# Four graph layers on one core: projections by one level of Strassen's algorithm over pairs of graphs, with every engine's order written by hand

## The chip, the core and the metric

The kernel runs on one core of a Trainium2 chip. The core has TensorE (PE in the profile; its weight loads are the row PEld), VectorE (DVE), ScalarE (ACT), GpSimd (POOL) and SyncE (SP), and 16 DMA engines. Each engine takes its own instructions in the order in which they stand in its queue, and semaphores order the engines against each other. The metric is device time in microseconds of one execution of the whole program. All data and all arithmetic are float32.

## The reference

There are 128 graphs of 128 nodes with 512 features. `x` is [128, 128, 512], `adj` is [128, 128, 128]. Four layers follow each other, each of them a residual with a layer normalisation, `LN(v) = (v - mean) / sqrt(var + 1e-5)` over the features:

```
An = D^-1/2 (adj + I) D^-1/2     with D the row sums of adj + I      (layers 0 and 3)
layer 0:  x = LN(x + relu(An x W0 + b0))
layer 1:  q, k = split(x Wqk^T)          v = x Wv^T
          w = softmax over nodes of sum_m (q k^T / 8 * adj)[n, m]
          x = LN(x + w * v)
layer 2:  agg = (adj x) / max(rowsum(adj), 1e-6)
          x = LN(x + relu([x, agg] W2^T))
layer 3:  x = LN(x + An (x W3 + b3))
```

W0, Wv and W3 are 512x512, W2^T is 1024x512, Wqk^T is 512x128. Per graph the projections are five products of [128, 512] by [512, 512]: one each in layers 0, 1 and 3 and two in layer 2.

## The kernel before, in words

Nodes lie on the 128 partitions. Four graphs make a group (G = 4), so there are 32 groups. The main loop runs `t` from 0 to 32; I call one turn of it a pass. In pass `t` group `t` goes through layers 0 and 1, and group `u = t - 1` through layers 2 and 3, so that two groups are in flight and one can fill the other's waits. `prep` for group `t + 1` sits in the middle of layer 3 of group `u`.

A layer is made of pieces. `aggregate` (L131) multiplies adjacency and features into a transposed result in a PSUM tile of pool `ps_t` (two buffers), four 128x128 products at a time, and ACT copies it to SBUF (L138). `transpose_x` (L141) does the same with the features alone (copy on L145). `project` (L147) takes four such chunks as the stationary operand and runs the weights past them, 512 columns at a time (L151), into one PSUM bank of `ps_big` (four buffers). DVE reads the bank, adds bias or applies the relu and adds the residual into a new tile of features (L184 and L185 for layer 0, L248 for layer 1, L265 for layer 2, L278 and L279 for layer 3). `stats` (L159) then takes the batch-norm statistics of that graph on DVE, and when the four graphs of the group are done `normalise` (L164) computes the reciprocal root for all four at once: a small DVE operation (L167), one power on POOL over 128x4 elements (L169), and four DVE operations in place (L171). A float32 product is two instructions on PE, a transpose is one.

The order of the instructions on each engine comes from the Tile framework, which starts from the order in the Python code and lets an instruction pass others on its engine (in the built program the row sums of `prep` for groups 1 and 2, for instance, stand on DVE ahead of layer 0 of group 0). ACT has only copies, the two scalings of q and k and the exponentials to do. POOL does the 160 small powers and issues the weight loads (L66, L71); SP issues the loads of `adj` and `x` (L55, L57) and the stores (L283).

Of the kernel before, what the change touches and what calls it, by code (L numbers as in the profile page):

```python
# [13 lines left out]
P = 128          # nodes of a graph, on the partitions  # L14
G = 4            # graphs handled together
F = 512          # features
C = F // P       # feature chunks of 128
ATT = 64
LN_EPS = 1e-5
DEG_EPS = 1e-6  # L20


@with_exitstack
def kernel(
# [4 lines left out]
    w0: bass.AP,      # [F, F]   in, out  # L29
    b0: bass.AP,      # [F]  # L30
    wqkT: bass.AP,    # [F, 2 * ATT]
    wvT: bass.AP,     # [F, F]   in, out
    w2T: bass.AP,     # [2 * F, F] in, out
    w3: bass.AP,      # [F, F]   in, out
    b3: bass.AP,      # [F]
# [7 lines left out]
    xp = ctx.enter_context(tc.tile_pool(name="xp", bufs=2))  # L43
    ap = ctx.enter_context(tc.tile_pool(name="ap", bufs=2))
    tp = ctx.enter_context(tc.tile_pool(name="tp", bufs=4))
    sp = ctx.enter_context(tc.tile_pool(name="sp", bufs=4))
    ps_big = ctx.enter_context(tc.tile_pool(name="ps_big", bufs=4, space=bass.MemoryType.PSUM))
    ps_t = ctx.enter_context(tc.tile_pool(name="ps_t", bufs=2, space=bass.MemoryType.PSUM))
    ps_s = ctx.enter_context(tc.tile_pool(name="ps_s", bufs=2, space=bass.MemoryType.PSUM))

    st = {}          # (name, group) -> tile

    def load(t):
        a = ap.tile([P, G, P], FP, tag="adj", name=f"adj_{t}", bufs=3)
        nc.sync.dma_start(a, adj[t * G:(t + 1) * G].rearrange("g n m -> n g m"))  # L55
        xi = xp.tile([P, G, F], FP, tag="x0", name=f"x0_{t}")
        nc.sync.dma_start(xi, x[t * G:(t + 1) * G].rearrange("g n f -> n g f"))  # L57
        st["adj", t], st["x0", t] = a, xi

# [1 line left out]
    load(0)  # L61

    def weight(src, name):
        n, m = src.shape
        w = const.tile([P, n // P, m], FP, tag=name, name=name)
        nc.gpsimd.dma_start(w, src.rearrange("(c p) m -> p c m", p=P))  # L66
        return w

# [11 lines left out]
    w0_sb = weight(w0, "w0_sb")  # L80
    b0_sb = broadcast_row(b0, "b0_sb")
    wqk_sb = weight(wqkT, "wqk_sb")
    wv_sb = weight(wvT, "wv_sb")
    w2_sb = weight(w2T, "w2_sb")
    w3_sb = weight(w3, "w3_sb")
# [6 lines left out]
    def prep(t):  # L92
# [3 lines left out]
        rdeg = sp.tile([P, G], FP, tag="rdeg", name=f"rdeg_{t}")  # L96
        nc.vector.tensor_scalar(rdeg, deg, DEG_EPS, None, ALU.max)
        nc.vector.reciprocal(rdeg, rdeg)
        ar = ap.tile([P, G, P], FP, tag="ar", name=f"ar_{t}")
        nc.vector.tensor_tensor(ar, a, per_graph(rdeg), ALU.mult)  # L100

# [4 lines left out]
        an = ap.tile([P, G, P], FP, tag="an", name=f"an_{t}")  # L106
        nc.vector.tensor_tensor(an, a, ident[:, None, :].to_broadcast([P, G, P]), ALU.add)
        nc.vector.tensor_tensor(an, an, per_graph(d), ALU.mult)

        p_r = ps_t.tile([P, G, P], FP, tag="pt", name=f"p_ar_{t}")  # L110
        for g in range(G):
            nc.tensor.transpose(p_r[:, g, :], ar[:, g, :], ident)  # L112
        arT = ap.tile([P, G, P], FP, tag="arT", name=f"arT_{t}", bufs=3)
        nc.scalar.copy(arT, p_r)
# [4 lines left out]
        nc.vector.tensor_tensor(anT, p_n, per_graph(d), ALU.mult)  # L119
        st["arT", t], st["anT", t] = arT, anT  # L120

    # row sums of An, which carry the bias of layer 3
    def row_sums(t):
        p = ps_s.tile([P, P], FP, tag="psm", name=f"p_rs_{t}")
        for g in range(G):
            nc.tensor.matmul(p[:, g:g + 1], st["anT", t][:, g, :], ones, start=True, stop=True)  # L126
        rs = sp.tile([P, G], FP, tag="rs", name=f"rs_{t}")
        nc.vector.tensor_copy(rs, p[:, :G])
        st["rs", t] = rs

# [1 line left out]
    def aggregate(name, t, g, xin, aT):  # L132
        """(A x)^T in chunks of 128 features, [f, node]."""
        p = ps_t.tile([P, C, P], FP, tag="pt", name=f"p_{name}_{t}_{g}")
        for c in range(C):
            nc.tensor.matmul(p[:, c, :], xin[:, g, c * P:(c + 1) * P], aT[:, g, :], start=True, stop=True)  # L136
        s = tp.tile([P, C, P], FP, tag="aggT", name=f"{name}_{t}_{g}", bufs=6)
        nc.scalar.copy(s, p)  # L138
        st[name, t, g] = s

    def transpose_x(name, t, g, xin, dst):  # L141
# [3 lines left out]
        nc.scalar.copy(dst, p)  # L145

    def project(name, t, g, parts):  # L147
        """sum over (lhsT chunks, weight chunks) -> PSUM [node, F]."""
        p = ps_big.tile([P, F], FP, tag="pb", name=f"p_{name}_{t}_{g}")
        for i, (lhsT, w) in enumerate(parts):  # L150
            nc.tensor.matmul(p, lhsT, w, start=(i == 0), stop=(i == len(parts) - 1))  # L151
        return p

    def new_x(name, t):
        z = xp.tile([P, G, F], FP, tag=name, name=f"{name}_{t}")
        mv = sp.tile([P, G, 2], FP, tag="mv" + name, name=f"mv{name}_{t}", bufs=2)
        st[name, t], st["mv" + name, t] = z, mv

    def stats(name, t, g):  # L159
        s = sp.tile([P, 6], FP, tag="bn", name=f"bn{name}_{t}_{g}")  # L160
        nc.vector.bn_stats(s, st[name, t][:, g, :])  # L161
        nc.vector.bn_aggr(st["mv" + name, t][:, g, :], s)  # L162

    def normalise(name, t):  # L164
        z, mv = st[name, t], st["mv" + name, t]
        ve = sp.tile([P, G], FP, tag="ve", name=f"ve{name}_{t}")
        nc.vector.tensor_scalar(ve, mv[:, :, 1], LN_EPS, None, ALU.add)  # L167
        r = sp.tile([P, G], FP, tag="rstd", name=f"rstd{name}_{t}")
        nc.gpsimd.tensor_tensor(r, ve, nhalf, ALU.pow)  # L169
        for g in range(G):  # L170
            nc.vector.tensor_scalar(z[:, g, :], z[:, g, :], mv[:, g, 0:1], r[:, g:g + 1],  # L171
                                    ALU.subtract, ALU.mult)

# [1 line left out]
    def l0_agg(t, g):  # L175
        aggregate("agg0", t, g, st["x0", t], st["anT", t])

    def l0_out(t, g):
        a = st.pop(("agg0", t, g))
        p = project("o0", t, g, [(a[:, c, :], w0_sb[:, c, :]) for c in range(C)])  # L180
        if g == 0:
            new_x("x1", t)
        z = st["x1", t][:, g, :]
        nc.vector.tensor_tensor(z, p, b0_sb, ALU.add)  # L184
        nc.vector.scalar_tensor_tensor(z, z, 0.0, st["x0", t][:, g, :], ALU.max, ALU.add)  # L185
        stats("x1", t, g)

# [1 line left out]
    def l1_xT(t, g):  # L189
        if g == 0:  # L190
            st["xT1", t] = tp.tile([P, C, G, P], FP, tag="xT1", name=f"xT1_{t}", bufs=2)
        transpose_x("xT1", t, g, st["x1", t], st["xT1", t][:, :, g, :])

    def l1_qk(t):
        xT = st["xT1", t]
        p = ps_t.tile([P, G * P], FP, tag="pt", name=f"p_qk_{t}")
        for c in range(C):
            nc.tensor.matmul(p, wqk_sb[:, c, :], xT[:, c].rearrange("p g n -> p (g n)"),  # L198
                             start=(c == 0), stop=(c == C - 1))
        qT = tp.tile([ATT, G * P], FP, tag="qT", name=f"qT_{t}", bufs=2)  # L200
        kT = tp.tile([ATT, G * P], FP, tag="kT", name=f"kT_{t}", bufs=2)
        nc.scalar.mul(qT, p[0:ATT, :], 1.0 / ATT ** 0.5)
        nc.scalar.copy(kT, p[ATT:2 * ATT, :])
        st["qk", t] = qT, kT

    def l1_scores(t):
# [3 lines left out]
        for g in range(G):  # L210
            s = slice(g * P, (g + 1) * P)
            nc.tensor.matmul(p[:, g, :], qT[:, s], kT[:, s], start=True, stop=True)  # L212
# [6 lines left out]
    def l1_softmax(t):  # L219
        p = ps_s.tile([P, P], FP, tag="psm", name=f"p_w_{t}")  # L220
# [13 lines left out]
    def l1_weights(t):  # L234
        p = ps_s.tile([P, P], FP, tag="psm", name=f"p_ws_{t}")
# [5 lines left out]
    def l1_v(t, g):  # L241
        xT = st["xT1", t]
        st["v", t, g] = project("v", t, g, [(xT[:, c, g, :], wv_sb[:, c, :]) for c in range(C)])

    def l1_out(t, g):
        if g == 0:
            new_x("x2", t)
        nc.vector.scalar_tensor_tensor(st["x2", t][:, g, :], st.pop(("v", t, g)), st["ws", t][:, g:g + 1],  # L248
                                       st["x1", t][:, g, :], ALU.mult, ALU.add)
        stats("x2", t, g)  # L250

# [1 line left out]
    def l2_in(t, g):  # L253
        aggregate("agg2", t, g, st["x2", t], st["arT", t])
        s = tp.tile([P, C, P], FP, tag="xT2", name=f"xT2_{t}_{g}", bufs=3)
        transpose_x("xT2", t, g, st["x2", t], s)
        st["xT2", t, g] = s

    def l2_out(t, g):
        xT, a = st.pop(("xT2", t, g)), st.pop(("agg2", t, g))  # L260
# [112 lines left out]
```

## Time and profile before

| | us |
|---|---|
| median of 3 runs | 2960.03 (2957.54 to 2961.9) |
| profiled execution, span of the core | 2958.7 |
| PE busy | 2896.0 (98%) |
| PEld busy (beside PE) | 1568.0 (53%) |
| DVE busy | 1396.0 (47%) |
| ACT busy | 425.7 (14%) |
| POOL busy | 167.5 (6%) |

The profiled execution's own time is the span from its first to its last instruction, and stands 1.3 us under the median of the runs. The page's groups give the busy time and the mean duration of an instruction, and behind the last bar how long its engine sat idle before it and what ended that. Matmuls are pipelined, so the mean duration of one is longer than the distance between two that follow each other; that distance is read from a row of the timeline, where a run of equal instructions is merged with its length. One pass of the loop takes about 2958.7 / 32 = 92.5 us.

### The profile page before, as it was taken

How to read it: one execution, taken by the hardware profiler on the slowest of the kernel's cores; microseconds unless marked ns; L12 is line 12 of the kernel's file. 1: busy time of each engine (PE TensorE's matmuls, PEld its weight loads, DVE VectorE, ACT ScalarE, POOL GpSimd, SP SyncE). 2: the span in 40 equal slices, each digit the busy share in tenths (PEclk: the TensorE clock that was granted, in tenths of full speed). 3: DMA queues.
4: the chain of work that ended last, by engine and by line, in shares of the span. 5: the costliest groups of instructions: out<-in, count | busy, mean ns of one | idle time of the engine just before them, and what ended most of it. 6: DMA issues, size and time to landing. Idle time of an engine off the chain costs nothing.

```text
span 2958.7 us, 25787 instructions
## 1 busy us (share of the span) xinstructions
PE 2896.0 (98%) x10304; PEld 1568.0 (53%) x10304; DVE 1396.0 (47%) x3138; ACT 425.7 (14%) x801; POOL 167.5 (6%) x173
## 2 busy tenths in 40 slices
PE   5999999999999999999999999999999999999998
PEld 2555555555555555555555555555555555555554
DVE  2455444455444554444554445544445544455443
ACT  1111111111111111111111111111111111111110
POOL 1000000000000000000000000000000000000000
PEclk9999999999999999999999999999999999999998
DMA  4000000000000000000000100000000001000000
GB/s 139 18 29 32 18 18 32 29 32 23 13 33 29 32 32 18 18 32 29 32 19 18 32 29 33 32 18 18 32 29 32 18 18 32 29 32 15 15 1 29
DMA packets 52391, 83.18 MB, mean 28 GB/s; under 512 B 1648, under 2 KB 18032, under 8 KB 52272
## 3 DMA queue, kind: packets, MB, share of 16 engines
q1 hardware_dynamic: 50688, 75.50, 7.4%
q0 software_dynamic: 1584, 6.03, 0.6%
q8 instruction: 82, 1.34, 0.2%
q14 instruction: 37, 0.30, 0.0%
HBM read 47.97 MB, written 33.55 MB: 28 GB/s over the span
## 4 chain that ended last, share of the span: by engine, by line
PE 97%; DMA 1%; ACT 1%; DVE 1%; issue 0%; POOL 0%; SPq 0%; POOLq 0%; ACTq 0%; DVEq 0%
PE p_o L151 60%; PE p_v L151 15%; PE p_agg L136 12%; PE p_qk L198 4%; PE p_xT L144 3%; PE p_sc L212 1%; DMA adj<-in_adj_dram 1%; PE p_rs L126 1%; ACT agg L138 1%; PE p_an L117 0%; PE p_ar L112 0%; PE p_ws L236 0%; PE p_w L221 0%; DVE x L171 0%; DVE bnx L161 0%
## 5 line engine op out<-in xcount | busy, mean ns | idle before, releaser
L151 PE MATMUL p_o<-w_sb,agg 128*128 128x512 f32 x3072 | 1381.5, 594 | 0.1
L151 PEld LDWEIGHTS p_o<-w_sb,agg 128*128 128x128 f32 x3072 | 566.9, 190 | 630.2 <-issue 629.0
L138 ACT COPY agg<-p_agg 128x512 f32<-128x512 f32 x384 | 225.1, 586 | 1730.9 <-PE p_agg L136 1730.9
L151 PE MATMUL p_v<-wv_sb,xT 128*128 128x512 f32 x1024 | 466.5, 600 | 0.0
L151 PE MATMUL p_o<-w_sb,xT 128*128 128x512 f32 x1024 | 465.8, 593 | 0.0
L265 DVE SCALAR_TENSOR_TENSOR x<-p_o,x 128x512 f32<-128x512 f32 x128 | 88.5, 691 | 782.5 <-PE p_o L151 782.5
L161 DVE BATCH_NORM_STATS2 bnx<-x 128x6 f32<-128x512 f32 x512 | 348.2, 690 | 12.1
L171 DVE TENSOR_SCALAR x<-x,mvx,rstdx 128x512 f32<-128x512 f32 x512 | 245.2, 542 | 151.5 <-POOL rstdx L169 151.5
L136 PEld LDWEIGHTS p_agg<-anT,x 128*128 128x128 f32 x2048 | 259.5, 194 | 83.4 <-issue 83.4
L151 PEld LDWEIGHTS p_v<-wv_sb,xT 128*128 128x128 f32 x1024 | 186.9, 190 | 213.5 <-issue 209.0
L136 PE MATMUL p_agg<-anT,x 128*128 128x128 f32 x2048 | 265.8, 278 | 6.5 <-DVE x L171 3.8
L151 PEld LDWEIGHTS p_o<-w_sb,xT 128*128 128x128 f32 x1024 | 182.2, 190 | 169.3 <-issue 169.3
L169 POOL TENSOR_TENSOR rstdx<-vex,nhalf 128x4 f32<-128x4 f32 x128 | 129.3, 1010 | 2462.6 <-DVE vex L167 2462.6
L145 ACT COPY xT<-p_xT 128x512 f32<-128x512 f32 x256 | 144.7, 590 | 212.3 <-PE p_xT L144 212.3
L136 PEld LDWEIGHTS p_agg<-arT,x 128*128 128x128 f32 x1024 | 131.8, 191 | 62.4 <-issue 45.9
L184 DVE TENSOR_TENSOR x<-p_o,b_sb 128x512 f32<-128x512 f32 x128 | 88.3, 690 | 157.9 <-PE p_o L151 157.9
L278 DVE SCALAR_TENSOR_TENSOR x<-b_sb,rs,p_o 128x512 f32<-128x512 f32 x128 | 95.6, 747 | 140.8 <-PE p_o L151 140.8
L144 PE MATMUL p_xT<-ident,x 128*128 128x128 f32 x1024 | 144.1, 274 | 4.4 <-DVE x L171 4.4
L136 PE MATMUL p_agg<-arT,x 128*128 128x128 f32 x1024 | 138.2, 278 | 9.1 <-ACT agg L138 9.1
L144 PEld LDWEIGHTS p_xT<-ident,x 128*128 128x128 f32 x1024 | 120.8, 142 | 39.4 <-issue 30.5
L198 PE MATMUL p_qk<-xT,wqk_sb 128*128 128x512 f32 x256 | 115.2, 592 | 0.0
L162 DVE BATCH_NORM_AGGREGATE mvx<-bnx 128x2 f32<-128x6 f32 x512 | 90.3, 179 | 13.1
(54 smaller groups left out, 879.5 us busy)
## 6 DMA issues: line engine op xcount, KB each, us to landing
x<-in_x_dram SPq DMA_DIRECT2D x32, 1024.0 KB, 5.3
out_dram<-x SPq DMA_DIRECT2D x32, 1024.0 KB, 4.3
adj<-in_adj_dram SPq DMA_DIRECT2D x32, 256.0 KB, 2.8
w_sb<-in_L_gnn_W_dram POOLq DMA_DIRECT2D x1, 2048.0 KB, 20.3
w_sb<-in_L_gnn_kernel_dram POOLq DMA_DIRECT2D x1, 1024.0 KB, 8.7
wv_sb<-in_L_gnn_W_v_dram POOLq DMA_DIRECT2D x1, 1024.0 KB, 13.4
w_sb<-in_L_gnn_W_dram POOLq DMA_DIRECT2D x1, 1024.0 KB, 22.5
b_sb<-in_L_gnn_bias_dram POOLq DMA_DIRECT2D x1, 256.0 KB, 9.3
```

Source lines behind the costliest of these rows:

```text
L136: nc.tensor.matmul(p[:, c, :], xin[:, g, c * P:(c + 1) * P], aT[:, g, :], start=True, stop=True)
L138: nc.scalar.copy(s, p)
L144: nc.tensor.transpose(p[:, c, :], xin[:, g, c * P:(c + 1) * P], ident)
L145: nc.scalar.copy(dst, p)
L151: nc.tensor.matmul(p, lhsT, w, start=(i == 0), stop=(i == len(parts) - 1))
L161: nc.vector.bn_stats(s, st[name, t][:, g, :])
L162: nc.vector.bn_aggr(st["mv" + name, t][:, g, :], s)
L169: nc.gpsimd.tensor_tensor(r, ve, nhalf, ALU.pow)
L171: nc.vector.tensor_scalar(z[:, g, :], z[:, g, :], mv[:, g, 0:1], r[:, g:g + 1], ALU.subtract, ALU.mult)
L198: nc.tensor.matmul(p, wqk_sb[:, c, :], xT[:, c].rearrange("p g n -> p (g n)"), start=(c == 0), stop=(c == C - 1))
L265: nc.vector.scalar_tensor_tensor(st["x3", t][:, g, :], p, 0.0, st["x2", t][:, g, :], ALU.max, ALU.add)
L278: nc.vector.scalar_tensor_tensor(z, b3_sb, st["rs", t][:, g:g + 1], p, ALU.mult, ALU.add)
```

## The change

Four things change together.

First, `project` works on all four graphs of a group at once. Graphs 0 and 1 and graphs 2 and 3 form two pairs (index `q`), the graph within the pair is the row block `r`, and the halves of the 512 features are the column blocks. One level of Strassen's algorithm in Winograd's form replaces eight block products by seven: B11, T2, B21, T3, T1, T4, B22. Each product is four matmuls per weight matrix (two pairs, two chunks of 128 features) with 256 columns instead of 512. Three regions of PSUM per call (pool `ps_b`, five buffers) accumulate across products, and DVE adds regions and SBUF blocks between them. So a call of `project` in layers 0, 1 and 3 has 28 matmuls of 256 columns, and in layer 2 it has 56.

Second, the sums of left operands (`left_sums`, four operations of 128x512 per call) are made on POOL, five calls a pass, and the sums of weight blocks (`weight_sums`) once at the start, on DVE for W0 and on POOL for the other four matrices. The weights are loaded in four parts each, those of W0 from ACT's queue.

Third, a group's features stay in one tile (`xp`, four buffers) that each layer updates in place. `norm_stats` replaces `stats` and `normalise`: it is called twice per `project`, for two graphs each, and its last step, the scaling and shifting of the features, is an ACT operation in place. The PSUM pools are `ps_b` with five and `ps_t` with three buffers.

Fourth, `tc.manual_schedule()` keeps each engine's instructions in the order of the Python code. That code is rearranged: hooks put the transposes, q and k, the scores and the softmax of layer 1 between products of layer 2; `prep` is split into `prep_rows` (before layer 1's projection) and `prep_transpose`, and the aggregation of the next group's layer 0 stands before layer 3's projection. Layer 3's bias is added to the features ahead of its projection (`l3_bias`).

The diff, cut to what the text speaks of:

```diff
-    xp = ctx.enter_context(tc.tile_pool(name="xp", bufs=2))
+    xp = ctx.enter_context(tc.tile_pool(name="xp", bufs=4))
...
-    ps_big = ctx.enter_context(tc.tile_pool(name="ps_big", bufs=4, space=bass.MemoryType.PSUM))
-    ps_t = ctx.enter_context(tc.tile_pool(name="ps_t", bufs=2, space=bass.MemoryType.PSUM))
-    ps_s = ctx.enter_context(tc.tile_pool(name="ps_s", bufs=2, space=bass.MemoryType.PSUM))
+    ps_b = ctx.enter_context(tc.tile_pool(name="ps_b", bufs=5, space=bass.MemoryType.PSUM))
+    ps_t = ctx.enter_context(tc.tile_pool(name="ps_t", bufs=3, space=bass.MemoryType.PSUM))
+
+    ctx.enter_context(tc.manual_schedule())
...
+    def left_sums(name, t):
+
+        a = st[name, t].rearrange("p (q r) (h c) n -> p q r h c n", r=2, h=2)
+        a11, a12, a21, a22 = a[:, :, 0, 0], a[:, :, 0, 1], a[:, :, 1, 0], a[:, :, 1, 1]
+        s1, s2, s3, s4 = (tp.tile([P, 2, 2, P], FP, tag=f"s{i}", name=f"{name}s{i}_{t}", bufs=3) for i in (1, 2, 3, 4))
+        nc.gpsimd.tensor_tensor(s1, a21, a22, ALU.add)
+        nc.gpsimd.tensor_tensor(s2, s1, a11, ALU.subtract)
+        nc.gpsimd.tensor_tensor(s3, a11, a21, ALU.subtract)
+        nc.gpsimd.tensor_tensor(s4, a12, s2, ALU.subtract)
+        st[name, t] = {B11: a11, B21: a12, B22: s4, T4: a22, T1: s1, T2: s2, T3: s3}
...
+    def project(name, t, parts, first, c11, fin, hooks=None):
...
+        g1 = region()
+        product(g1, B11, True)
+        sa, sb = first(g1, block)
+        v = region()
+        product(v, T2, True)
+        u2 = block("u2")
+        nc.vector.tensor_tensor(u2, v, sb, ALU.add)
+        product(g1, B21, False)
+        c11(g1, block)
+        product(v, T3, False)
+        u3 = block("u3")
+        nc.vector.tensor_tensor(u3, v, sb, ALU.add)
+        q_ = region()
+        product(q_, T1, True)
+        nc.vector.tensor_tensor(u3, q_, u3, ALU.add)
+        fin(1, 1, u3)
+        product(v, T4, False)
+        nc.vector.tensor_tensor(sa, v, sa, ALU.add)
+        fin(1, 0, sa)
+        norm_stats(name, t, 1)
+        product(q_, B22, False)
+        nc.vector.tensor_tensor(u2, q_, u2, ALU.add)
+        fin(0, 1, u2)
+        norm_stats(name, t, 0)
...
+    def copy_first(p, block):
+        s = block("s")
+        nc.scalar.copy(s, p)
+        return s, s
...
+    def norm_stats(name, t, r):
+        z = st["x", t]
+        mv = sp.tile([P, 2, 2], FP, tag="mv", name=f"mv{name}_{t}_{r}")
+        for q in range(2):
+            s = sp.tile([P, 6], FP, tag="bn", name=f"bn{name}_{t}_{r}_{q}")
+            nc.vector.bn_stats(s, z[:, 2 * q + r, :])
+            nc.vector.bn_aggr(mv[:, q, :], s)
+        ve = sp.tile([P, 2], FP, tag="ve", name=f"ve{name}_{t}_{r}")
         nc.vector.tensor_scalar(ve, mv[:, :, 1], LN_EPS, None, ALU.add)
...
+        rstd = sp.tile([P, 2], FP, tag="rstd", name=f"rstd{name}_{t}_{r}")
+        nc.gpsimd.tensor_tensor(rstd, ve, nhalf[:, 0:2], ALU.pow)
+        nmr = sp.tile([P, 2], FP, tag="nmr", name=f"nmr{name}_{t}_{r}")
+        nc.vector.scalar_tensor_tensor(nmr, mv[:, :, 0], -1.0, rstd, ALU.mult, ALU.mult)
+        for q in range(2):
+            zg = z[:, 2 * q + r, :]
+            nc.scalar.activation(zg, zg, AF.Identity, bias=nmr[:, q:q + 1], scale=rstd[:, q:q + 1])
...
+        if a:
+            l0_out(t)
         if b:
+            l2_in(u)
...
+        if a and b:
+            l2_out(u, {B11: scores, B21: lambda: l1_scores(t), T1: lambda: l1_softmax(t),
+                       B22: lambda: l1_weights(t)})
...
+        if t + 1 < NT:
+            prep_rows(t + 1)
+        if a:
+            l1_out(t)
         if b:
+            l3_agg(u)
+            row_sums(u)
+            l3_bias(u)
+        if t + 1 < NT:
+            prep_transpose(t + 1)
+            l0_agg(t + 1)
         if b:
+            l3_out(u)
             store(u)
```

In the new code `l2_in` issues, graph by graph, an aggregation and a transposition into `ps_t`, each copied by ACT; `scores` is `l1_xT`, `l1_qk` and the left sums of layer 1; `l3_agg` and `l0_agg` are four aggregations with their copies and then their left sums. `first` in layer 0 is two DVE additions of the bias, in the other layers the ACT copy `copy_first`; `fin` is one DVE operation of 128x512 (in layer 1 two of 128x256).

## The prediction

> **What bounds the kernel now.** I read the page's busy times and its chain first, then its groups, and last two stretches of the timeline.
>
> ```profile
> PE 2896.0 (98%) x10304; PEld 1568.0 (53%) x10304; DVE 1396.0 (47%) x3138; ACT 425.7 (14%) x801; POOL 167.5 (6%) x173
> ...
> PEclk9999999999999999999999999999999999999998
> ...
> PE 97%; DMA 1%; ACT 1%; DVE 1%; issue 0%; POOL 0%; SPq 0%; POOLq 0%; ACTq 0%; DVEq 0%
> ...
> L151 PE MATMUL p_o<-w_sb,agg 128*128 128x512 f32 x3072 | 1381.5, 594 | 0.1
> ...
> L138 ACT COPY agg<-p_agg 128x512 f32<-128x512 f32 x384 | 225.1, 586 | 1730.9 <-PE p_agg L136 1730.9
> ...
> L161 DVE BATCH_NORM_STATS2 bnx<-x 128x6 f32<-128x512 f32 x512 | 348.2, 690 | 12.1
> ...
> L169 POOL TENSOR_TENSOR rstdx<-vex,nhalf 128x4 f32<-128x4 f32 x128 | 129.3, 1010 | 2462.6 <-DVE vex L167 2462.6
> ...
> L184 DVE TENSOR_TENSOR x<-p_o,b_sb 128x512 f32<-128x512 f32 x128 | 88.3, 690 | 157.9 <-PE p_o L151 157.9
> ...
> L162 DVE BATCH_NORM_AGGREGATE mvx<-bnx 128x2 f32<-128x6 f32 x512 | 90.3, 179 | 13.1
> ```
>
> PE is the bound: 97% of the chain, full clock, projections idle for 0.1 us. Everybody else waits for PE, ACT's copies for 1730.9 us. The other rows are the prices used below.
>
> The timeline of the last group, where no second group fills the waits, shows what a normalisation costs PE when PE has to wait for it:
>
> ```profile
> 2924.07 0.69 DVE L265 SCALAR_TENSOR_TENSOR x<-p_o,x 128x512 f32<-128x512 f32 x1 [5.23 <-PE p_o L151]
> ...
> 2926.05 1.01 POOL L169 TENSOR_TENSOR rstdx<-vex,nhalf 128x4 f32<-128x4 f32 x1 [31.21 <-DVE vex L167]
> ...
> 2927.79 3.76 PE L136 MATMUL p_agg<-anT,x 128*128 128x128 f32 x16 [3.76 <-DVE x L171]
> ...
> 2931.34 4.40 PE L151 MATMUL p_o<-w_sb,agg 128*128 128x512 f32 x8
> ...
> 2935.57 1.05 PE L136 MATMUL p_agg<-anT,x 128*128 128x128 f32 x8
> ...
> 2936.46 3.60 PE L151 MATMUL p_o<-w_sb,agg 128*128 128x512 f32 x8
> ```
>
> and busy time by stretches around it (time, PE, PEld, DVE, ACT, POOL, granted clock, DMA) shows what the wait does to the clock:
>
> ```profile
> 2922.68:2926.09 3.41, 1.35 (x4) 0.28 (x2) 1.74 (x4) 0.00 (x0) 0.04 (x1) 1.00 0.00 0
> 2926.09:2929.51 3.42, 1.72 (x8) 1.75 (x9) 1.92 (x4) 0.00 (x0) 0.97 (x1) 0.50 0.00 0
> 2929.51:2932.92 3.41, 3.41 (x12) 2.50 (x12) 0.00 (x0) 1.17 (x2) 0.00 (x0) 0.50 0.00 0
> ```
>
> PE stands 3.76 us until the chain of DVE, POOL and DVE is through, and for 6.83 us the clock is 0.50. The eight matmuls of 512 columns took 4.40 instead of 3.60 us, and sixteen of 128, which take 2.03 us in the middle of the run (at 1514.65), took 3.76: 2.5 us lost behind the wait. After the 4.42 us wait at 58.39 us the same comparison gives about 1.8.
>
> **The matmuls.** From 3.60 us for eight, the last lasting 0.594: (3.60 - 0.594) / 7 = 0.429 us from start to start at 512 columns; (1.05 - 0.278) / 7 = 0.110 at 128. No row has 256 columns; between those two lies 0.217, and I take 0.216 (ends: 0.2145, half of 0.429, and 0.25, if the weight load of 0.190 should not hide quite; at 128 columns it hides within 0.110, so I stay near the low end). Per pass the projections go from 80 matmuls x 2 instructions x 0.429 = 68.6 us to 140 x 2 x 0.216 = 60.5 us. The rest of PE's pass is unchanged: 96 aggregation instructions, 16 for scores and row sums and 40 transposes at about 0.11, eight of q and k at 0.429, together 20.6 us. So PE's work falls from 89.2 to 81.1 us a pass, 8.1 us, and 32 x 8.1 = 260 us would be the gain (about 2700 us) if nothing else changed.
>
> **The tail of a projection.** What is added is a chain at the end of every `project`. From the end of T4 on PE (0.2 us until DVE starts): two DVE operations of 0.69 (sum, `fin`), twice 0.69 + 0.18 for the statistics, 0.17 for `ve`, 1.01 on POOL with 0.2 of hand-over, 0.17 for `nmr`, 0.2 of gaps: 5.0 us. DVE waits for POOL in its order, so only then does it take up B22's result: the same again, 4.9 us. Then two ACT operations on 128x512 at 0.59, 1.25 us. That is 11.2 us after T4's end. Only B22 runs beside it, 8 x 0.216 = 1.73 us, so the normalisations are through 9.5 us after the projection's last matmul. In the old order the same work was one DVE, POOL, DVE chain per group with another group's matmuls over it. Now the chain stands ahead of the next stage's work on ACT and DVE, because both keep the written order, and that work is not optional for PE:
>
> - Layer 0 to `l2_in`: its eight ACT copies are queued behind layer 0's four normalisations. PE may fill three `ps_t` buffers (0.90 + 0.44 + 0.90 = 2.2 us) and then waits for the first copy (0.62): 9.5 + 0.6 - 2.2 = 7.9 us. Behind it 1.4 us at q and k, whose last transposes wait for copies at 0.62 each.
> - Layer 2 to layer 1's projection: `copy_first` stands on ACT behind layer 2's normalisations. Here B22 has 3.46 us, so they end 7.8 us after it; with 0.6 for the copy, less B11 and T2 (3.5 us), B21 waits 5.0 us, and T3 another 0.5 for DVE, which has `prep_rows` ahead of `u2`.
> - Layer 1 to `l3_agg`: as the first case with three aggregations (2.7 us) to issue: 7.6 us.
> - `prep_transpose` to `l0_agg`: `anT` stands on DVE behind layer 1's tail, the row sums and `l3_bias`, four operations of 0.75: 3.3 us.
> - Layer 3 to layer 0's projection: `first` is two DVE operations behind `nmr` of layer 3 (8.2 us after the end); 8.2 + 1.45 less 3.46 of B11 and T2: 6.2 us.
>
> Together 32.4 us a pass with 0.5 of small ones, and 81.1 + 32.4 = 113.5 us.
>
> **The clock.** Four of these waits are over 3.76 us. At 1.8 to 2.5 us each they would add 7 to 10 us; the fifth wait, set by DVE, shrinks where PE is slower, as do the parts that go at the pace of ACT's copies. I take 6 us (ends 0 and 10): 119.5 us a pass. [...]
>
> **POOL's sums.** Twenty operations of 128x512 a pass, which no row shows. Below: DVE's 0.69. Above: 2.0, twice the 1.01 that POOL takes for the power. Up to about 1.5 they are done before PE asks: `l2_in`'s eight run from 1 us after the last copies, and T2 of layer 2 comes 10 us after these, behind B11, layer 1's transposes and q and k; layer 3's sums have the row sums, `prep_transpose` and `l0_agg` over them. I take 1.2, no cost; at 2.0 layer 2's T2 waits about 3.7 us a pass. [...]
>
> **The power over 128x2** is a new form: 1.01 is the row for 128x4, which I keep as nearest; below it 0.10 (the shortest POOL row, a fill of one column). At 0.5, each of four tails is 1 us shorter: 4 us a pass.
>
> **Edits that cost nothing.** DVE's sum rises to about 55 us a pass and ACT's to 26, far below 113. Loads: SP has the store of group u - 1 before the load of t + 1, and that store waits for ACT some 9.5 us into the pass; `prep_rows` needs `adj` at 64 us, and landing took 2.8 and 5.3 us. If that cover went, it would be some 8 us a pass. Four more `x` buffers and in-place layers put no wait on PE beyond the copies named. At the start POOL issues 19 weight loads and has 16 weight sums ahead of the first power: PE's real work began at 34.6 us before; I add 36 us for start and first weights (ends 30 and 50).
>
> **The sum.** Pass 0 (layers 0 and 1) 66, pass 1 about 115, 29 passes at 119.5 = 3465, the last with a `prep` missing 111, the drain pass 70 and 11 of final tail and store: 3838, with 36 in front 3874; against a profiled 2958.7 that is +915. The median of the runs stood 1.3 us over it. I say 3870.
>
> **The rivals.**
> 1. The waits are there, but the clock holds or the small power is short. For: at 58.39 and 2926 the clock fell, yet only there. Against: the same rows. 113.5 a pass gives 3690; with a power of 0.5 as well, 109.5, 3560; at 0.1 some 3430.
> 2. POOL's sums gate layer 2 or slow DVE down: at 2.0 us about 122 to 126 a pass, 3960 to 4100. For: the power's 1.01 for four elements speaks of a slow engine. Against: a 128x128 select on POOL took 0.30.
> 3. Faster: the tails lie under PE's work after all, say because a hand-made order lets copies and next products pass them. It decides where waits sum to under 8.1 + 3.3 us (what the old pass had beyond PE's work) instead of 32.4, that is where a projection's tail ends within about 4 us of its last matmul, not 9.5. Then 2700 to 2950. Against: ACT's and DVE's order in the built program has the normalisations first, and the 3.76 us wait above is a shorter chain.
> 4. The change does not do what it says: matmuls of 256 columns cost 0.25, bound by weight loads. 280 x 0.034 = 9.5 us a pass, some 4150.
>
> **Chances.** Forecast 0.50 (3750 to 3950), first rival 0.27, second 0.13, fourth 0.05, faster 0.045. The range leaves out the fourth, the ends of the second and faster: 3450 to 4070. 0.2% is about what a measurement of this kernel tells from no change: faster 0.045, same 0.005, slower 0.95.
>
> **What would show it.** PE busy near 70% with waits released by ACT copies of `agg` and `xT` and by layer 0's `first`, 5 to 8 us each, four per pass; PEclk at 8 or 9 throughout; 0.216 between matmuls of 256 columns; ACT's longest idle time ended by `nmr`. I am wrong if ACT copies start before the normalisations ahead of them, if a tail after T4 takes much less than 11 us, or if PE waits mostly for POOL.

## The result and the profile after

The changed kernel takes 3909.81 us (median of 4 runs, 3909.25 to 3910.91) beside 2960.78 us of the kernel before: a ratio of 1.321, with a 95% interval of 1.319 to 1.323. The profiled execution has a span of 3908.2 us, 1.6 us under that median. The forecast was 3870 us, in a range of 3450 to 4070.

These lines of the changed kernel's page answer to those shown of before: busy times, granted clock, the chain, and the groups with the long idle times (the number behind the last bar).

```profile
PE 3019.0 (77%) x14144; PEld 2601.0 (67%) x14144; DVE 1695.6 (43%) x3750; ACT 856.1 (22%) x1409; POOL 1069.7 (27%) x969
...
PEclk8888888888888888888888888888988889888898
...
PE 59%; DVE 23%; ACT 6%; POOL 6%; issue 6%; DMA 0%; ACTq 0%; POOLq 0%; DVEq 0%
...
L250 ACT ACTIVATE x<-x,nmro,rstdo 128x512 f32<-128x512 f32 x384 | 291.4, 806 | 1358.5 <-DVE nmro L247 1358.5
...
L245 POOL TENSOR_TENSOR rstdo<-veo,nhalf 128x2 f32<-128x2 f32 x192 | 134.3, 699 | 1571.5 <-DVE veo L243 1571.5
```

PE was 97% of the chain and is 59%; DVE, POOL, ACT and "issue" (time with no cause in the profile) have taken up the rest. The clock is between 8 and 9 tenths in every slice.

PE's own waits, by what ended them (total over the run, number, longest):

```profile
PE p_xT L165 <- ACT agg L159: 215.6, 32, 6.7
PE p_agg L158 <- ACT agg L159: 200.6, 31, 6.5
PE p_o L191 <- DVE s_o L274: 140.8, 30, 4.7
PE p_agg L158 <- issue: 119.4, 30, 4.0
PE p_v L191 <- ACT s_v L231: 108.7, 31, 3.5
PE p_qk L294 <- ACT xT L166: 25.8, 32, 0.8
```

Each happens once a pass, so the longest is also the usual one. In the order of the pass they are layer 0 to `l2_in` (6.7 us), q and k (0.8), layer 2 to layer 1's projection (3.5), layer 1 to `l3_agg` (6.5), `prep_transpose` to `l0_agg` (4.0), layer 3 to layer 0 (4.7): 26.2 us a pass.

One of these places in the timeline of the changed kernel, the end of layer 1's projection (start, length, engine, line and operation, and in brackets the idle time before it):

```profile
1752.28 2.84 PE L158 MATMUL p_agg<-anT,x 128*128 128x128 f32 x24
...
1759.29 0.16 DVE L247 SCALAR_TENSOR_TENSOR nmrv<-mvv,rstdv 128x2 f32<-128x2 f32 x1 [0.81 <-POOL rstdv L245]
1759.55 1.52 ACT L250 ACTIVATE x<-x,nmrv,rstdv 128x512 f32<-128x512 f32 x2 [2.79 <-DVE nmrv L247]
1760.97 1.53 ACT L159 COPY agg<-p_agg 128x512 f32<-128x512 f32 x3
1761.59 2.08 PE L158 MATMUL p_agg<-anT,x 128*128 128x128 f32 x8 [6.46 <-ACT agg L159]
...
1765.40 4.85 DVE L371 SCALAR_TENSOR_TENSOR x<-b_sb,rs,x 128x512 f32<-128x512 f32 x4
1765.66 1.71 POOL L175 TENSOR_TENSOR agg3s<-agg 128x512 f32<-128x512 f32 x1
...
1767.33 1.71 POOL L176 TENSOR_TENSOR agg3s<-agg,agg3s 128x512 f32<-128x512 f32 x1
...
1770.17 0.68 DVE L132 TENSOR_TENSOR anT<-p_an,d 128x512 f32<-128x512 f32 x1
1770.95 1.41 PE L158 MATMUL p_agg<-anT,x 128*128 128x128 f32 x5 [3.98 <-issue]
```

PE fills three buffers with aggregations (24 matmuls) and has finished them at 1755.1 us. ACT could copy the first of them by then, but in its written order layer 1's four normalisations come first, and the last two of these wait for `nmrv` until 1759.45. Only at 1760.97 does ACT copy. Then PE comes to a second wait: `anT` stands on DVE behind the four bias operations.

The distance of two passes, taken from the first DVE sum of layer 0, is 119.7 to 121.3 us, 120.4 in the mean. It divides into 26.2 us in which PE is idle (the waits above; the trace has no other idle time inside a pass), a loss to the half clock of 11.5 (worked out below), and what is left, 82.7, for PE's work at full clock. At half clock eight matmuls of 128 columns take 2.08 us (from 1761.59, above), at full clock 1.05 (from 1807.49): work at half clock takes twice its time.

### The profile page after: what moved, and what is told of

It reads as the page before. It is cut to its first block, busy times and chain, and to the rows that moved or that the text cites. A ratio compares the mean times of both kernels' runs of the same rounds, so it can differ in the third digit from the quotient of the medians.

```text
span 3908.2 us, 35734 instructions
## 1 busy us (share of the span) xinstructions
PE 3019.0 (77%) x14144; PEld 2601.0 (67%) x14144; DVE 1695.6 (43%) x3750; ACT 856.1 (22%) x1409; POOL 1069.7 (27%) x969
## 3 DMA queue, kind: packets, MB, share of 16 engines
q10 hardware_dynamic: 1088, 1.05, 0.1%
## 4 chain that ended last, share of the span: by engine, by line
PE 59%; DVE 23%; ACT 6%; POOL 6%; issue 6%; DMA 0%; ACTq 0%; POOLq 0%; DVEq 0%
PE p_o L191 33%; PE p_agg L158 9%; PE p_v L191 7%; DVE bno L240 6%; POOL rstdo L245 3%; PE p_qk L294 3%; ACT x L250 3%; PE p_xT L165 2%; DVE x L262 2%; DVE bnv L240 2%; DVE mvo L241 2%; DVE s_o L217 2%; ACT xT L166 2%; DVE u_o L221 1%; DVE x L342 1%
## 5 line engine op out<-in xcount | busy, mean ns | idle before, releaser
L250 ACT ACTIVATE x<-x,nmro,rstdo 128x512 f32<-128x512 f32 x384 | 291.4, 806 | 1358.5 <-DVE nmro L247 1358.5
L191 PE MATMUL p_o<-w_sb,agg 128*128 128x256 f32 x1536 | 419.3, 422 | 140.8 <-DVE s_o L274 140.8
L206 DVE TENSOR_TENSOR u_o<-p_o,s_o 128x512 f32<-128x512 f32 x64 | 44.3, 691 | 971.4 <-PE p_o L191 971.4
L191 PEld LDWEIGHTS p_o<-w_sb,agg 128*128 128x128 f32 x1536 | 320.4, 213 | 201.2 <-DVE s_o L274 152.8
L191 PE MATMUL p_o<-w2x_sb,xT2s 128*128 128x256 f32 x1024 | 266.8, 383 | 0.0
L191 PE MATMUL p_o<-w2a_sb,agg2s 128*128 128x256 f32 x1024 | 263.8, 380 | 3.9 <-POOL agg2s L174 3.9
L240 DVE BATCH_NORM_STATS2 bno<-x 128x6 f32<-128x512 f32 x384 | 260.3, 678 | 6.5
L191 PE MATMUL p_o<-w_sb,agg0s 128*128 128x256 f32 x1024 | 258.5, 404 | 3.3 <-POOL agg0s L174 3.3
L191 PE MATMUL p_v<-wv_sb,xT1s 128*128 128x256 f32 x1024 | 259.0, 405 | 0.0
L191 PEld LDWEIGHTS p_v<-wv_sb,xT1s 128*128 128x128 f32 x1024 | 213.8, 209 | 37.0 <-issue 1.7
L191 PE MATMUL p_o<-w_sb,agg3s 128*128 128x256 f32 x1024 | 237.3, 380 | 1.1 <-DVE u_o L206 1.1
```

The costliest lines, as they stand in the source:

```text
L191: nc.tensor.matmul(p[:, q, :], left_[k][:, q, c, :], w[:, k, c, :], start=(fresh and q == 0 and i == 0 and c == 0), stop=(i == len(parts) ...
L240: nc.vector.bn_stats(s, z[:, 2 * q + r, :])
L250: nc.scalar.activation(zg, zg, AF.Identity, bias=nmr[:, q:q + 1], scale=rstd[:, q:q + 1])
```

## The experiments

All of them are edits of the changed kernel, or of the redone order below, and were compared with the kernel before on the same chip, which took 2960 to 2962 us each time. The redone order was run four times, each of the others once. The theory is that of the prediction: nothing in the arithmetic is slow; the scalings and shifts on ACT and the tails on DVE stand ahead of work for PE, in an order that the engines must keep.

### Letting the scheduler order the same instructions

```diff
-    ctx.enter_context(tc.manual_schedule())
```

> The changed kernel with the one line removed that keeps every engine's order as written; the Tile framework may again let instructions pass each other on their engine. In the changed kernel a pass of 120.3 us is 81.1 of PE work at full clock, 27.1 of PE waits and 12 lost to half clock. Theory (the written order puts the tail of a normalisation ahead of copies that PE needs): most of the waits go and the clock with them, 85 to 98 us a pass, 2750 to 3150 us in all. Rival (the seven products and their block sums need these waits in any order, because the operands come late): it stays above 3500 us. Second rival (the matmuls of 256 columns are the loss): no change, 3900.

Measured 3026.32 us, 883 us less with the same instructions. A pass is 92.2 us, and PE is busy for 2741.7 us (91%); its largest wait that recurs is 2.3 us a pass, ended by DVE's sum `u_o`. So the loss against this order, 883 us, is one of order alone. Strassen's form with this order is still 2% slower than the kernel before.

### Only ACT's order changed

ACT's scalings and shifts are collected and issued behind the next stage's copies; DVE, POOL and PE keep their order.

```diff
-        for q in range(2):
-            zg = z[:, 2 * q + r, :]
-            nc.scalar.activation(zg, zg, AF.Identity, bias=nmr[:, q:q + 1], scale=rstd[:, q:q + 1])
+        def shift():
+            for q in range(2):
+                zg = z[:, 2 * q + r, :]
+                nc.scalar.activation(zg, zg, AF.Identity, bias=nmr[:, q:q + 1], scale=rstd[:, q:q + 1])
+        late.append(shift)
...
+    def flush():
+        while late:
+            late.pop(0)()
```

> The changed kernel with one thing moved: the ACT operations that scale and shift the features after a projection are issued behind the next stage's ACT copies (behind the eight copies ahead of layer 2, behind the copy of layer 1's first region, behind the copies for the next group's layer 0) instead of ahead of them. DVE, POOL and PE keep their order and all their work. Theory: the three waits that ACT copies end (6.7, 6.5 and 3.5 us a pass) go, with about 7 us of the half-clock loss; the waits that DVE ends (layer 0's first region 4.7, the next group's aggregation 4.0) stay: about 96 us a pass, 3050 to 3250 us, and PE's waits then name DVE. Rival (ACT only seems to be the cause, and the chain through DVE and POOL holds PE whichever way ACT is ordered): at most 100 us less, above 3800.

Measured 3508.92 us: 401 us gained where I expected 660 to 860. Waits of PE in this kernel:

```profile
PE p_agg L158 <- issue: 280.3, 30, 9.4
PE p_o L191 <- DVE s_o L285: 140.7, 30, 4.7
PE p_v L191 <- DVE u_v L206: 110.3, 31, 3.7
```

The two waits for ACT's `agg` copies, 13.2 us a pass together, are gone, but the one ahead of `l0_agg` has grown from 4.0 to 9.4 us, and the wait for `s_v` on ACT (3.5) has become one for `u_v` on DVE (3.7). The first of these has no cause in the profile ("issue"), as in the changed kernel, where PE starts 0.1 us after `anT` is through. At both places DVE's tail stood right behind ACT's, so that taking away the first only showed the second.

### Keeping the clock up without removing a wait

PE multiplies weights into a spare region (7, 7, 5 and 4 products of 512 columns at four of the waits, each two instructions on PE), so that it isn't idle there; nothing else is changed.

```diff
+    def keep_busy(name, t, n):
+        p = region(name, t)
+        for _ in range(n):
+            nc.tensor.matmul(p, ident, w0_sb[:, B11], start=True, stop=True, skip_group_check=True)
+        early.append(p)
...
```

> The changed kernel with extra matmuls of 512 columns on PE, whose results are overwritten and never used: seven before the fourth group of products ahead of layer 2 and seven before the fourth aggregation of layer 3 (6.0 us each at 0.858 for a float32 product), five and four before the third product of layers 0 and 1 (4.3 and 3.4 us). They fill PE's waits and shorten none. Theory (of the 39 us that a pass has beyond PE's work, about 12 are half clock behind the waits): the clock stays near 1.0, the waits' ends stay where DVE and ACT put them, and a pass falls to about 113 us, 3650 to 3720 us in all, with more work on PE. Rival (the half clock runs in time in which PE would wait anyway): within 50 us of 3910.

Measured 3681.61 us, mean granted clock 0.964 instead of 0.861. So about 228 us of the loss, 7.1 us a pass, is the half clock behind the waits, net of what the added work delays. The trace agrees: PE's busy time at half clock falls from 738 to 126 us, and half of the difference is 306 us. The rest of the loss is the waits themselves.

### Making a tail longer

```diff
         nc.gpsimd.tensor_tensor(rstd, ve, nhalf[:, 0:2], ALU.pow)
+        nc.gpsimd.tensor_tensor(rstd, ve, nhalf[:, 0:2], ALU.pow)
```

> The changed kernel with the small power on POOL done twice in each normalisation, the second over the first, so that the result comes about 0.7 us later; POOL has time for it (27% busy). Theory (every wait of PE hangs on the tail of sum, statistics, POOL and DVE, twice in a row): each of the four tails becomes 1.4 us longer, a pass 5.6 us longer at full clock and up to 8 with the half clock, 4080 to 4160 us in all. Rival (POOL's small power is off PE's path, hidden by DVE's other work): within 20 us of 3910.

Measured 4097.01 us. The four waits that I had put down to a tail grew, from 6.7 to 8.3, 6.5 to 8.0, 4.7 to 6.2 and 3.5 to 5.1 us, each by about two powers of 0.70 us: the chain of two halves, each with its DVE part, its power and its way back, does set the end of all four.

### POOL's sums, doubled and left out

```diff
         nc.gpsimd.tensor_tensor(s1, a21, a22, ALU.add)
+        if name in ("xT2", "agg2"):
+            nc.gpsimd.tensor_tensor(s1, a21, a22, ALU.add)
```

and the same for `s2`, `s3` and `s4`.

> The changed kernel with POOL's eight left sums of layer 2 each done twice. In the changed kernel the sixth of them is through 2.1 us before T2 of layer 2 needs it; twice as long, at 1.27 us each, it comes 5.3 us after that. Theory (POOL's sums cost nothing at their size, with 2.1 us to spare): a new wait of T2 of about 5.3 us a pass, ended by POOL's agg2s, 3908 + 164 = 4070 us, up to 4140 with half-clock time behind it. Rival (the sums are not near the path at all): within 15 us of 3908.

Measured 4201.39 us. The new wait is there and has the size expected (`agg2s` ends 187.1 us of PE's waits, 5.8 a pass), but the price is 292 us, 9.4 a pass, above my 4070 to 4140: PE's busy time rose by another 106 us, since the matmuls behind this wait too run at half clock (its busy time at half clock goes from 738 to 940 us). The reading on the path holds: the sums cost no wait as they are, with 2.1 us to spare, and the gating of the prediction's second rival would have begun at sums of about 1.6 us (1.27 + 2.1 / 6, since the sixth is the one that T2 needs).

```diff
-        left_sums("agg3", t)
+        a = st["agg3", t].rearrange("p (q r) (h c) n -> p q r h c n", r=2, h=2)
+        a11, a12, a21, a22 = a[:, :, 0, 0], a[:, :, 0, 1], a[:, :, 1, 0], a[:, :, 1, 1]
+        st["agg3", t] = {B11: a11, B21: a12, B22: a22, T4: a22, T1: a21, T2: a11, T3: a21}
```

> The changed kernel without POOL's four left sums of layer 3 (blocks of the aggregation stand in for the sums, so layer 3's projection has other operands and the output is not the reference's). Nothing waited for these sums. Theory that POOL's additions slow DVE where both DVE inputs are in SBUF: the four operations of layer 3's bias, 1.27 us in the mean beside those sums, go to 0.74 each, anT comes 2.1 us earlier, the wait of PE at the next group's aggregation (4.0 us a pass) falls to some 1.9, and 31 passes give 60 to 70 us, with a little less half-clock time 3815 to 3860 us. Rival, that the bias is slow by itself (its broadcast operand, its place): 1.27 us and 3895 to 3915 us.

Measured 3878.6 us. Without POOL's sums beside them, the bias operations take 0.75 us in the mean instead of 1.27, and the wait at `l0_agg` falls from 4.0 to 1.9 us, both as the theory says; the rival falls. But only 31 us came out of the 63 by which the waits shrank, less than the 50 to 95 that I expected. Why is seen in stretches of 3.41 us (time, then the busy time and the instructions of PE, PEld, DVE, ACT and POOL, then the granted clock and DMA) behind the wait of layer 1, first in the changed kernel:

```profile
1760.41:1763.82 3.41, 2.23 (x11) 2.23 (x11) 0.00 (x0) 2.21 (x5) 1.26 (x1) 0.50 0.00 0
1763.82:1767.24 3.42, 3.15 (x15) 2.75 (x14) 2.00 (x3) 0.70 (x2) 2.81 (x2) 0.50 0.00 0
1767.24:1770.65 3.41, 0.00 (x0) 0.00 (x0) 3.41 (x4) 0.35 (x1) 1.80 (x2) 0.50 0.00 0
1770.65:1774.06 3.41, 3.11 (x15) 3.14 (x16) 0.20 (x1) 0.58 (x1) 0.00 (x0) 0.52 0.00 0
1774.06:1777.48 3.42, 3.42 (x26) 3.27 (x26) 0.00 (x0) 1.75 (x3) 0.62 (x1) 1.00 0.00 0
```

and without layer 3's sums:

```profile
1743.41:1746.82 3.41, 1.82 (x8) 1.82 (x9) 0.00 (x0) 2.51 (x5) 0.00 (x0) 0.55 0.00 0
1746.82:1750.24 3.42, 3.42 (x18) 3.17 (x16) 1.59 (x4) 0.59 (x1) 0.00 (x0) 0.50 0.00 0
1750.24:1753.65 3.41, 1.54 (x7) 1.43 (x7) 1.91 (x3) 0.59 (x1) 0.00 (x0) 0.50 0.00 0
1753.65:1757.06 3.41, 3.41 (x18) 3.41 (x17) 0.00 (x0) 1.17 (x2) 0.00 (x0) 0.50 0.00 0
1757.06:1760.48 3.42, 3.42 (x22) 3.19 (x21) 0.00 (x0) 1.38 (x3) 1.27 (x1) 0.95 0.00 0
```

In these two passes the clock stays at 0.50 for the same time, four stretches. Where the second wait is 2.1 us shorter, PE works 2.1 us longer at half speed in them, which gets 1.05 us of work done: 30 passes of it are the 31 us. In most other passes of the changed kernel the half clock lasts five stretches here, so the whole run is the better sum: PE's busy time at half clock rises from 738 to 809 us, and half of the 71 us, 36, is lost again.

That a changed wait is worth half of its length is not a rule. With the doubled power PE's idle time grew by 196 us and the run by 187, nearly all of it, since the time at half clock hardly changed (738 to 722 us); with the doubled sums 185 us more of idle time cost 292, since the time at half clock rose to 940.

### The hand order, redone on both engines

The work is the same and the manual schedule stays. On ACT all scalings stand behind the next copies, as above. On DVE layer 3's bias and both its statistics move into the next pass, behind layer 2's input; layer 2's second statistics go behind layer 1's first products; layer 1's first statistics go behind its last sum, their `nmr` and the second statistics behind `anT`; `prep_rows` moves into layer 2. `norm_stats` is divided for this into `stats` (up to the power) and a part that finishes. On POOL the third and fourth left sums of layers 2 and 3 move back as well (behind the first two of the next call, and behind `anT`); what that is worth by itself no run shows.

```diff
+        if t >= 2:
+            l3_bias(t - 2)
+            both("o3", t - 2)
+            stores.append(t - 2)
...
+            if t + 1 < NT:
+                hooks[T3] = lambda: prep_rows(t + 1)
...
-            l1_out(t)
+            after["c11"] = lambda: held.append(stats("o2", u, 0))
+            after["r0"] = lambda: vr1.append(stats("v", t, 1))
+            l1_out(t, after)
...
-            l3_bias(u)
         if t + 1 < NT:
             prep_transpose(t + 1)
+        if vr1:
+            vr1.pop()()
+            stats("v", t, 0)()
```

> All work and the hand order kept as a hand order, but the order redone on ACT and DVE. ACT: every scaling and shifting stands behind the next stage's copies. DVE: layer 3's bias and both its statistics move behind the next pass's layer 2 input, the second half of layer 2's statistics behind layer 1's first products, layer 1's statistics behind the aggregation of layer 3 and behind anT; the row sums of prep move into layer 2. POOL: the third and fourth left sums of a call go behind the first two of the next. My theory: the waits of PE in the changed kernel are an effect of what stands ahead of the copies and sums on ACT and on DVE, both at once, and putting only ACT right moved them to DVE. Then PE has its 81.1 us a pass plus 3 to 6 us of small waits, the clock holds near 1, and the time is 2700 to 2850 us, under both kernels. Rival A: the tails are too long for any written order and POOL's sums beside DVE's slow it (1.3 instead of 0.74 us): waits ended by DVE or POOL of 10 us a pass and more remain, 2950 to 3250 us. Rival B: only a reordering by the scheduler can interleave that finely: not under 3026 us.

Measured 2794.13 us (median of 4 runs, 2793.17 to 2795.15), 0.944 of the kernel before with a 95% interval of 0.942 to 0.945. It beats both kernels and lies in the range expected. Its busy times and clock, from its page:

```profile
PE 2661.9 (95%) x14144; PEld 2296.7 (82%) x14144; DVE 1845.2 (66%) x3750; ACT 848.6 (30%) x1409; POOL 1089.8 (39%) x969
...
PEclk8899999999999999999999999999999999999999
```

its waits of PE that recur:

```profile
PE p_qk L332 <- ACT xT L166: 25.4, 32, 0.8
...
PE p_o L202 <- ACT s_o L244: 18.0, 31, 2.6
...
PE p_agg L158 <- issue: 11.8, 30, 0.4
```

and ACT's timeline at the place shown of the changed kernel:

```profile
1443.44 0.58 ACT L159 COPY agg<-p_agg 128x512 f32<-128x512 f32 x1 [0.31 <-PE p_agg L158]
1444.34 0.58 ACT L159 COPY agg<-p_agg 128x512 f32<-128x512 f32 x1 [0.31 <-PE p_agg L158]
1444.82 2.93 ACT L278 ACTIVATE x<-x,nmrv,rstdv 128x512 f32<-128x512 f32 x4
```

The same four normalisations now come after all eight copies of `l3_agg` and `l0_agg`, and ACT waits for PE (0.31 us) and no longer PE for ACT. A pass is 84.4 us with under 2 us of waits, so PE's work is about 82.6 us at full clock.

### The redone order with ACT put back, and under the scheduler

```diff
-            late.append(shift)
+            shift()
```

> The redone hand order with one thing put back: ACT's scaling and shifting stands right behind its nmr again, ahead of the next stage's copies where nmr is ahead of them. Theory of the two causes: layer 0's tail gates the next copies again (6.5 us a pass of waits ended by ACT's agg and xT copies), layer 2's first half gates layer 1's first copy by some 2 us, the rest stays away; with half-clock time behind the 6.5 us wait, 10 to 13 us a pass more than the redone order: 2980 to 3200 us, by waits ended by ACT, none over 3 us a pass ended by DVE. Rival (DVE's order is all that counts): within 60 us of the redone order.

Measured 3606.51 us, above my range.

```profile
PE p_xT L165 <- ACT xT L166: 310.7, 30, 10.4
PE p_xT L165 <- ACT agg L159: 208.9, 31, 6.7
PE p_agg L158 <- ACT agg L159: 89.3, 30, 3.0
```

Layer 0's wait came back with 6.7 us, as said. I had missed two others: layer 3's normalisations, which this order has moved into the next pass, now stood ahead of the `xT` copies for q and k (10.4 us), and layer 1's first ahead of `l0_agg`'s (3.0). ACT's part of the new order alone gained 401 us, the rest of it (DVE's and POOL's) alone 303, and all together 1116. At the places of the changed kernel the two queues are in series, so that the tail of one hides the other's, as the run with ACT's order showed; and the 303 are net of the two new waits, which the changed kernel does not have, so the three numbers are no sum of parts.

The other variant is the redone order without `tc.manual_schedule()`.

> The redone order with the scheduler let loose on it (the manual schedule left out). Theory that the order in the code is what costs: starting from a better order the scheduler does no worse than its 3026 us on the changed kernel, 2720 to 2950 us. Rival that the scheduler alone finds what it finds: 3000 to 3050 us from either start.

Measured 3048.22 us, as the rival says and above my 2720 to 2950. From a better order the scheduler makes a worse one, with a wait of 6.5 us a pass at q and k for ACT's `xT` copies: a place that the hand order leaves at 0.8.

## Why the prediction came out as it did

The forecast was 1% under the measurement. The mechanism held, the places of the waits and what ends them; that the number came so close is in part luck, since two of its terms were off by some 6 us a pass, one each way.

**PE's work** was put at 81.1 us a pass and is about 82.7. The price of a 256-column matmul held: eight take 1.89 us with the last lasting 0.379, so (1.89 - 0.379) / 7 = 0.216. The fourth rival (0.25) is out. The shortfall was there before the change: the kernel before was busy for 2896.0 / 32 = 90.5 us a pass, where the prediction has 89.2. (The prediction's own terms for the unchanged part, 152 x 0.11 + 8 x 0.429, give 20.2 and not 20.6.) At full clock, that is PE's busy time less half of what lies at half clock, PE's work fell from 2892 to 2650 us, 242 instead of 260.

**The waits**, the step that carries the forecast, came at all the six places named. Five are put down by the profile to the instruction named; the one ahead of `l0_agg` has no cause there ("issue"), but ends 0.1 us after `anT` (1770.17 + 0.68, against 1770.95). The extra 0.5 us for DVE in layer 1 did not come. ACT's longest idle time is ended by `nmr`. Their sum is 26.2 us instead of 32.4 (31.9 at these places and 0.5 of small ones; the 7.6 at `l3_agg` should be 7.4 by the prediction's own terms):

| place | predicted | measured |
|---|---|---|
| layer 0 to `l2_in` | 7.9 | 6.7 |
| q and k | 1.4 | 0.8 |
| layer 2 to layer 1 | 5.0 and 0.5 | 3.5 |
| layer 1 to `l3_agg` | 7.6 | 6.5 |
| `prep_transpose` to `l0_agg` | 3.3 | 4.0 |
| layer 3 to layer 0 | 6.2 | 4.7 |

The term that was too large is the tail, 11.2 us after T4 by the prediction. In layer 0 at 1804 it takes 10.2: T4 ends at 1805.9 and the last scaling at 1816.1. The power over 128x2 takes 0.70 us, not 1.01 (twice 0.3); the hand-over between DVE and POOL and the gaps are shorter than the 0.4 us put in for each half; against this ACT's two operations take 1.52 us, not 1.25, since one with a scale and a bias per partition is 0.76 to 0.81 us and a copy 0.59. The one wait that was too small, at `l0_agg`, has the four bias operations at 4.85 us instead of 3.0 (4 x 0.75): the experiment without layer 3's sums, which brings them to 0.75 each and the wait to 1.9, shows that POOL's additions beside them are the cause.

**The clock** was put at 6 us a pass with 10 as the upper end, and costs 11.5. Over the whole run, 738 us of PE's busy time lies at half clock, 23.0 us a pass in the mean, and half of that is lost. In the pass from 1736 on, the four stretches of half clock last 3.4, 13.7, 6.8 and 6.8 us, with 3.4, 8.3, 4.8 and 5.1 us of PE's work in them. The step that failed is the reduction from "7 to 10" to 6, by the thought that other waits shrink where PE is slower: the waits ahead of `l3_agg` and `l0_agg` fell into one long stretch instead, which costs 4.2 us here, more than the 1.8 to 2.5 taken for a wait, and the wait of 3.5 us mostly brought the clock down too.

All changes of the clock in the changed kernel lie on one grid of 3.413 us, to within 0.3 us, wherever the waits fall. Cut on that grid, two passes with the same wait of 3.5 us at layer 1's projection (from 1618.74 and from 1738.35) look like this, the columns as above with GB/s at the end:

```profile
1616.89:1620.30 3.41, 1.85 (x9) 1.29 (x7) 2.46 (x8) 0.62 (x2) 0.69 (x1) 1.00 0.00 0
1620.30:1623.72 3.42, 1.47 (x7) 1.31 (x8) 3.21 (x8) 1.90 (x3) 1.01 (x1) 1.00 0.00 0
1623.72:1627.13 3.41, 3.41 (x17) 2.81 (x16) 1.84 (x4) 0.00 (x0) 0.00 (x0) 1.00 0.00 0
...
1739.76:1743.17 3.41, 1.31 (x6) 1.18 (x7) 3.20 (x9) 1.99 (x3) 1.01 (x1) 1.00 0.00 0
1743.17:1746.58 3.41, 3.41 (x10) 2.67 (x9) 1.30 (x3) 0.00 (x0) 0.00 (x0) 0.50 0.00 0
```

Behind 1.47 us of PE's work in such a stretch the clock held, behind 1.31 it fell. From 290 to 3800 us of this trace it fell behind stretches with at most 1.45 us of work and held behind those with at least 1.45; in the run with filled waits 1.60 still let it fall. So the wait of 3.5 us brought the clock down in 24 of the 30 passes from 290 us on, and not in six. Each of these six saves half of a 3.4 us stretch, 1.7 us. All 116 longer waits from 290 to 3800 us (4.0 to 6.7 us) had half clock behind them.

So the waits were 6.2 us too long, the half clock 5.5 us and PE's work 1.6 us too short, and the errors nearly cancelled: 82.7 + 26.2 + 11.5 = 120.4 us a pass against 119.5. With the waits alone sized right the forecast would have been some 190 us lower (30 x 6.2), near 3680.

**POOL's sums** were taken at 1.2 us, an estimate between 0.69 and 2.0, with no cost to PE's path. They take 1.26 us where nothing disturbs them, and the doubling shows that 2.1 us were to spare. That they slow DVE was named in the second rival and not priced; it is real: without layer 3's sums the waits are 2.1 us a pass shorter and the run 1 us a pass.

**The ends**: layer 0 of pass 0 begins at 33.2 us (36 was put in front), pass 0 takes 77.6 instead of 66 and the last two together 186 instead of 192.

**The rivals.** The first (the clock holds) is refuted by the clock itself; the run with filled waits, at 3682 us, shows what a clock that nearly holds (0.964) is worth. The third (faster) named the right turning point, waits under 11.4 us a pass, and the right means, a hand-made order that lets copies pass the tails. The changed kernel has no such order. The redone one has, with under 2 us of waits, and lands within the 2700 to 2950 given for it.

## What to carry to other kernels

An algorithm that saves 8% of the bound engine's work (2892 to 2650 us here) is worth that only if nothing stands in front of that engine; before writing an order by hand, list for every wait of the bound engine all that is queued ahead of its releaser, on each engine in the chain, for a change on one queue shows only a part of its worth until the other is put right as well (401 of 1116 us here). Where a wait is long enough to bring PE's clock down (3.5 us was in 24 of 30 passes here), price the half clock from stretches of the timeline, with the work that lies in them, over several passes and not one; a changed wait is worth its length plus half of the change in PE's time at half clock, which came to between half and 1.6 times its length here. And a tail that nobody needs soon can go into the next pass, as long as it is moved on every engine that takes part in it.

## What the runs showed of the hardware beyond that

**Layer 3's bias operations on DVE are slow beside POOL's additions, and these are slow too.** The bias operation of layer 3, with `b_sb` and `x` in SBUF, takes 0.74 us alone; beside POOL's additions half of them take 1.75 in the changed kernel (1.27 in the mean) and three of four in the redone order (1.45), and POOL's addition then 1.71 instead of 1.26. A sum with one input in PSUM, such as `u_o` from `p_o` and `s_o`, takes 0.69 either way (61 of these 64 at L206 of the changed kernel run beside an addition). In the redone order the bias stands beside layer 2's sums, and the slowness moved with it: `agg2s` and `xT2s` go to 1.7 us, `agg3s` back to 1.27, and even `nmr`, over 128x2, takes up to 1.22 us beside an addition and 0.16 without; `ve`, with one input, goes from 0.17 to 0.73 and 0.82 there (at 1484.57 and 1486.94). From 1479 on in the redone order the ends alternate, POOL at 1479.02, DVE at 1479.57, POOL at 1480.69, DVE at 1481.24, POOL at 1482.36, DVE at 1482.92. Each DVE operation ends 0.55 us after POOL's and each addition 1.12 after DVE's. Some of the work ran at the same time: in the 5.78 us from 1477.13 on in the redone order, DVE did four bias operations (3.0 us alone) and POOL additions that take 4.2 alone, which is 7.2 us of work. By the distances of the ends I estimate 0.19 us of each bias operation (0.74 - 0.55) and 0.15 of each addition (1.27 - 1.12). Why the two are slow beside each other no run shows.

**The clock comes back by stretches of time.** The half clock lasted 3.4, 6.8, 10.2, 13.7 or 17.1 us in the changed kernel (34, 42, 16, 9 and 22 times; once, at the start, 23.9), whole steps of 3.41 us. PE's busy time alone does not say when it ends: in the stretches listed for the changed kernel above, under the run without layer 3's sums, one with 3.15 us of it (from 1763.82) did not end the half clock, and one with 3.11 us (from 1770.65) did. The first has most of the row sums in it, matmuls of a single column (1.71 us from 1763.46 by the trace); whether that decides was not tested.
